# Decoder on one core: keys and values of two cross attentions computed behind the expert tiles, and rows loaded back block by block

## The chip, the cores and the metric

The kernel runs on one core of a Trainium2 chip. A core has five engines that each take their own queue of instructions: TensorE (PE in the profile, with its weight loads as PEld), VectorE (DVE), ScalarE (ACT), GpSimd (POOL) and SyncE (SP), which here issues most of the DMA transfers. The metric is the device time of one execution in microseconds (us). The kernel before has a median of 1467.24 us over 3 runs (1461.73 to 1477.14).

## The reference

The model is a decoder of four layers with layer norms behind each residual sum. The input is 32 sequences of 64 tokens with 128 features, all float32. Each layer has a self attention, a cross attention to a context of the same shape, and a third part that differs: a local transformer (layer 0), routed experts (layers 1 and 2), a linear layer with float8 rounding (layer 3). Every layer runs the same three lines with other functions:

```python
x = _layernorm(x + attn(x))
x = _layernorm(x + xattn(x, ctx_1024))
x = _layernorm(x + ffn(x))
```

The change concerns the cross attentions of layers 2 and 3 and what stands ahead of each layer's self attention. The cross attention of layer 2, cut down (the one of layer 3 has two masks and no output projection):

```python
qh = (q @ Wq.T + bq).reshape(B, S, H, Hd).transpose(0, 2, 1, 3)   # q is x, H = 16, Hd = 8
kh = (k @ Wk.T + bk).reshape(B, S, H, Hd).transpose(0, 2, 1, 3)   # k is ctx_1024
vh = (v @ Wv.T + bv).reshape(B, S, H, Hd).transpose(0, 2, 1, 3)   # v is ctx_1024
attn = softmax(einsum('bhqd,bhkd->bhqk', qh, kh) / sqrt(Hd))
out = einsum('bhqk,bhkd->bhqd', attn, vh).transpose(0, 2, 1, 3).reshape(B, S, D) @ Wo.T + bo
```

Keys and values depend on the context and the weights alone, not on x. The experts of layer 1 send each token to one of eight feed-forward networks; those of layer 2 do the same with room for 80 tokens per expert and weigh the result with the gate's probability.

## The kernel before

**Tiling.** The 2048 tokens lie in 4 blocks of 512 (8 sequences). A block's x has 4 tiles of 128 tokens; xT is the same block turned, with the features on the partitions. The parts of the layers carry names: `l1f` are the experts of layer 1, `l2a` and `l2x` the self and cross attention of layer 2, `l2f` its experts, `l3a` and `l3x` the attentions of layer 3, `l3f` the last linear layer.

**Order.** A list of steps sets TensorE's order by hand: `sp.at(step, place, f)` puts a piece of work at a step and a place in it, and all pieces run sorted by the two. The order of the other engines comes from a scheduler that follows dependencies. SyncE and GpSimd issue the DMAs in their own queues.

**Attention (`attn8`, L618).** A block has 4 score tiles n of 4 sequences and 8 heads each. In a step TensorE makes s(n) from `kx` and q (and, in l2a, the alibi table; in l3a and l3x, a mask); VectorE takes the maximum (L598) and subtracts it; ScalarE makes the exponential (L601). Two steps later TensorE turns p (L612), ScalarE copies it as pT (L614), and TensorE multiplies it with v to o, whose ninth column holds the sum. Between s, the turn of p and o stand, at place 4, the projections of the next block: `prepare` (L640) runs K, Q, V in three successive steps. K is copied by ScalarE (L542, L544) and multiplied with a head mask into two `kx` tiles by GpSimd (L549; this instruction is `self.wide`); for block 0 of a self attention VectorE makes one of the two. V is copied by ScalarE (L564) into one of two constant tiles `v8` with ones in the ninth columns, set up at the start (L392 to L394). Each block ends with the output projection `y`, the residual sum, and a layer norm: statistics on VectorE (L468, L469), rstd on GpSimd (L423, L338), x on GpSimd (L483) or on ScalarE (L490, with `nb`, L488, from VectorE).

**Experts (`sorted_experts` L1301, `capacity_experts` L1441).** 23 tiles of l1f and 8 of l2f run one behind the other. Each scatters its result rows to DRAM by a GpSimd DMA. The last sum of a tile is `y` on VectorE. `wbig`, [128, 8 x 1156] floats, holds the weights of the experts; those of l2f, three transfers for each of the 8 experts (w1 and w2 of 256 KB each, and b2), are asked for while l1f's last tiles run.

**Between the experts and the next attention.** The result rows come back by block as z(b) (`load_after`, L1252). z(0) waits for all scatters. The loads of z(1), z(2) and z(3) are issued behind each other at one step, and wait for `kx` of block 0 as well. `added` sums z and x and normalises: block 0's x half by VectorE, half by ScalarE, all later ones by ScalarE with `nb` from VectorE. `turn_x` (L494) turns x on TensorE and copies xT on ScalarE (L501). In steps counted from the first score of the next self attention, blocks 1, 2 and 3 are added and turned at steps 0, 2 and 4:

```python
back, later = [(n - 4, 3.5), (n, 2), (n + 2, 6), (n + 4, 6)], (n - 1, 2)
```

Of the kernel before, what the change touches and what calls it, by code (L numbers as in the profile page):

```python
# [273 lines left out]
class Decoder:  # L274
# [66 lines left out]
    def setup(self):  # L341
# [48 lines left out]
        for n in range(2):  # L390
            v = self.const([P, BPB, 8, 2, 9], f"v8_{n}")
            nc.gpsimd.memset(v, 0.0)  # L392
            nc.gpsimd.memset(v[0:64, :, :, 0, 8:9], 1.0)
            nc.gpsimd.memset(v[64:128, :, :, 1, 8:9], 1.0)  # L394
            self.v8.append(v)

    def clear(self, sp, first):
# [96 lines left out]
    def turn_x(self, blk, part=(0, TPB)):  # L494
        t0, n = part
        ps = self.ps8("G", "xTps")
        for t in range(n):
            self.nc.tensor.transpose(ps[:, t * P : (t + 1) * P], self.xt[blk][:, t0 + t, :], self.ident)
        if t0 == 0:
            self.xT[blk] = self.const([P, TB], "xT", bufs=5)  # L500
        self.nc.scalar.copy(self.xT[blk][:, t0 * P : (t0 + n) * P], ps[:, 0 : n * P])  # L501


    def attn8_prep(self, blk, w, src, rope, scale, bqs, quick):

# [22 lines left out]
        def q_part():  # L528
            qT = got["q"] = self.q2([P, TB], "q8")
            if rope is not None:  # L530
                turned("wq", "bq", self.xT[blk], rope[:, 0:128], qT)
            elif "bq" in w:
                nc.scalar.activation(qT, proj("wq", self.xT[blk]), AF.Identity, bias=bqs, scale=scale)
            else:
                nc.scalar.mul(qT, proj("wq", self.xT[blk]), scale)

        def k_part():
            kT = self.q2([P, TB], "k8")
            if rope is not None:
                turned("wk", "bk", src(blk), rope[:, 128:256], kT)  # L540
            elif "bk" in w:
                nc.scalar.activation(kT, proj("wk", src(blk)), AF.Identity, bias=w["bk"], scale=1.0)  # L542
            else:
                nc.scalar.copy(kT, proj("wk", src(blk)))  # L544
            got["k"] = []
            for i in range(2):
                kx = self.q4([P, 2, TB], "kx")
                eng = nc.vector if quick and i else nc.gpsimd
                self.wide = eng.tensor_tensor(  # L549
                    out=kx, in0=bc(kT, 1, 2), in1=bc(head[:, 2 * i : 2 * i + 2], 2, TB), op=ALU.mult  # L550
                ).ins
                got["k"].append(kx)

        def v_part():
            x = src(blk)
            p3 = self.ps8("G", "vps").rearrange("p (b h d) -> p b h d", h=8, d=8)
            wv = w["wv"].rearrange("p (h u d) -> p h u d", u=2, d=8)
            for b in range(BPB):
                for u in range(2):
                    self.mm(p3[64 * u : 64 * u + 64, b], x[:, b * S : (b + 1) * S], wv[:, :, u, :])  # L560
            v = got["v"] = self.v8[blk % 2]
            for u in range(2):
                r = slice(64 * u, 64 * u + 64)
                nc.scalar.copy(v[r, :, :, u, 0:8], p3[r])  # L564

        return got, (k_part, q_part, v_part)

# [49 lines left out]

    def attn8(self, sp, base, name, src=None, rope=None, scale=1.0, row=None, mask=(None, None), has_out=True, split=False, number=False):  # L618

# [19 lines left out]

        def prepare(blk, i):  # L640
            if i == 0:
                prep[blk] = self.attn8_prep(blk, setup["w"], src, rope, scale, setup.get("bqs"), quick and blk == 0)
            prep[blk][1][i]()

# [72 lines left out]

        sp.at(base - 4, 3, start)
        for blk in range(NBLK):
            for i in range(3):  # L720
                sp.at(base + 4 * blk - 4 + i, 4, lambda blk=blk, i=i: prepare(blk, i))
            sp.at(base + 4 * blk + 2, 5.5, lambda blk=blk: resid(blk))
# [577 lines left out]

    def sorted_experts(self, sp, name, ready, fetched, tiles, back, later):  # L1301

# [90 lines left out]
        def second(j):  # L1393
# [6 lines left out]
            y = ys[j // 4][:, j % 4, :]  # L1400
            self.tt(y, ps[:, 0:D], w2[:, 4 * P + 4 :], ALU.add)
            at = xg[j // 3].bitcast(U32)[:, j % 3, D : D + 1]
# [15 lines left out]
        def rows_back(b):  # L1418
            z[b] = self.q2([P, TPB, D], "z")
            self.load_after(z[b], self.token_rows(0, b), k["y"] + ([self.wide] if b else []))  # L1420

# [11 lines left out]
        sp.at(tiles[-1][0], tiles[-1][1] + 0.05, lambda: rows_back(0))  # L1433
        for b in range(1, NBLK):
            sp.at(*later, lambda b=b: rows_back(b))
        for b in range(NBLK):
            sp.at(*back[b], lambda b=b: added(b))
            sp.at(back[b][0], back[b][1] + 0.1, lambda b=b: self.turn_x(b))


    def capacity_experts(self, sp, name, ready, fetched, tiles, back, later):  # L1441
        nc = self.nc
# [41 lines left out]
        def second(e):  # L1484
# [23 lines left out]
        def rows_back(b):  # L1508
            z[b] = self.q2([P, TPB, D], "z")
            self.load_after(z[b], self.token_rows(1, b), k["y"] + ([self.wide] if b else []))  # L1510

# [10 lines left out]
        )  # L1522
        sp.at(*fetched, fetch)
# [4 lines left out]
        for b in range(1, NBLK):  # L1528
            sp.at(*later, lambda b=b: rows_back(b))
        for b in range(NBLK):  # L1530
            sp.at(*back[b], lambda b=b: added(b))
            sp.at(back[b][0], back[b][1] + 0.1, lambda b=b: self.turn_x(b))

# [150 lines left out]
def decoder_kernel(ctx: ExitStack, tc: tile.TileContext, ins, at, out):  # L1684
# [63 lines left out]
```

## Time and profile before

| | us |
|---|---|
| median of 3 runs (lowest, highest) | 1467.24 (1461.73, 1477.14) |
| the profiled execution | 1467.96 |
| its span in the profile | 1466.2 |
| TensorE busy | 1228.0 (84%) |
| VectorE, ScalarE, GpSimd busy | 929.0, 694.1, 737.6 |
| mean granted clock of TensorE | 0.889 |

The profile comes from one execution. Its span is the time from the first to the last instruction; 1.8 us lie around it. A row names the source line, the engine, the operation, the tiles out<-in, the shape and how often it ran. "Granted clock" is the share of full speed that TensorE's throttle allowed. In square brackets stand the idle time before a row and the instruction that ended it. The last expert tile of l1f ends at 953, that of l2f at 1212; l2a and l2x lie between the two, l3a, l3x and the last linear layer behind the second.

### The profile page before, as it was taken

To read this page: it belongs to the slowest core of one execution; us is meant where nothing else is said; L and a number is where in the kernel's file an instruction comes from. 1 tells how busy PE (TensorE), PEld (TensorE's weight loads), DVE (VectorE), ACT (ScalarE), POOL (GpSimd) and SP (SyncE) were. 2 spreads that over 40 slices of the span, in tenths; PEclk is the share of its full clock that TensorE was granted. 3 is DMA by queue.
4 is the path that set the end of the run, shared out by engine and by line. 5 is a ranking of instruction groups with operands and counts; after the bars stand their busy time and mean duration, and the time that the engine had idled before them with its cause. 6 is when DMAs were issued, how large, how long until landed. Compare 5 with 4: busy or idle time off the path is not lost. (4 is left out here: it accounts for less than half of the span.)

```text
span 1466.2 us, 36930 instructions
## 1 busy us (share of the span) xinstructions
PE 1228.0 (84%) x16009; PEld 889.8 (61%) x16009; DVE 929.0 (63%) x1831; ACT 694.1 (47%) x1179; POOL 737.6 (50%) x609
## 2 busy tenths in 40 slices
PE   7997888889887898989889995939999853999880
PEld 4775555555555555656667775916677752677670
DVE  5754577777886776666564655635577435676765
ACT  2453444555554554554555542735565312556551
POOL 3534688677785755445542443523355232454531
PEclk9998899999999999999999975969999566999955
DMA  6001010360010000100010002230000001000000
GB/s 231 2 2 24 1 45 1 104 185 2 1 53 1 1 1 2 37 31 2 1 35 32 4 17 60 68 124 2 2 8 5 4 15 32 2 2 3 2 16 14
DMA packets 33714, 43.16 MB, mean 29 GB/s; under 512 B 5946, under 2 KB 27121, under 8 KB 33168
## 3 DMA queue, kind: packets, MB, share of 16 engines
q1 hardware_dynamic: 31536, 38.20, 8.1%
q8 instruction: 126, 2.06, 0.6%
q0 software_dynamic: 2016, 2.60, 0.6%
q14 instruction: 36, 0.29, 0.1%
HBM read 26.63 MB, written 15.56 MB: 29 GB/s over the span
## 5 line engine op out<-in xcount | busy, mean ns | idle before, releaser
L598 DVE TENSOR_REDUCE mx<-s 128x16 f32<-128x1024 f32 x96 | 117.4, 1223 | 127.0 <-PE s L335 125.6
L338 POOL TENSOR_TENSOR turn<-turn,turn 128x1024 f32<-128x1024 f32 x64 | 150.6, 2361 | 92.4 <-DVE turn L338 91.9
L338 DVE TENSOR_TENSOR p<-s,mx 128x1024 f32<-128x1024 f32 (+1 forms) x144 | 158.8, 1103 | 5.0
L614 ACT COPY pT<-ptps 128x512 f32<-128x512 f32 x192 | 104.7, 589 | 92.6 <-PE ptps L612 90.3
L601 ACT ACTIVATE p<-p 128x1024 f32<-128x1024 f32 x96 | 101.6, 1058 | 78.9 <-DVE p L338 77.6
L335 PEld LDWEIGHTS o<-v,pT 128*64 128x64 f32 x3072 | 109.3, 148 | 44.3 <-ACT pT L614 34.6
L549 POOL TENSOR_TENSOR kx<-k,w_const 128x1024 f32<-128x1024 f32 x45 | 85.4, 1917 | 97.8 <-ACT k L542 61.4
L335 PE MATMUL o<-v,pT 128*64 128x18 f32 x3072 | 120.8, 220 | 8.4 <-ACT pT L614 6.2
L335 PE MATMUL s<-kx,q 32*64 32x128 f32 x3072 | 114.6, 286 | 8.0 <-DVE sparts L1558 3.5
L423 POOL TENSOR_SCALAR rstd<-bnmv 128x4 f32<-128x4 f32 (+1 forms) x60 | 16.0, 267 | 198.9 <-DVE bnmv L469 152.5
L612 PE MATMUL ptps<-w_const,p 128*128 128x128 f32 x768 | 115.8, 299 | 0.2 <-ACT c L808 0.2
L335 PEld LDWEIGHTS s<-kx,q 32*64 32x64 f32 x3072 | 89.1, 138 | 44.0 <-issue 40.5
L338 DVE TENSOR_TENSOR turn<-qkps,w_const 128x512 f32<-128x512 f32 (+1 forms) x96 | 75.9, 862 | 53.6 <-PE qkps L335 53.6
L612 PEld LDWEIGHTS ptps<-w_const,p 128*128 128x128 f32 x768 | 96.3, 155 | 9.1 <-issue 8.2
L338 POOL TENSOR_TENSOR rn<-rn,nhalf 128x16 f32<-128x16 f32 x32 | 93.6, 2926 | 2.7
L857 PE MATMUL ropeT<-w_const,turn 128*128 128x128 f32 x512 | 71.1, 285 | 26.2 <-ACT oT L915 12.5
L857 PEld LDWEIGHTS ropeT<-w_const,turn 128*128 128x128 f32 x512 | 58.8, 145 | 39.0 <-ACT oT L915 12.0
L338 DVE TENSOR_TENSOR turn<-qkps,xtab 128x512 f32<-128x512 f32 (+1 forms) x96 | 82.1, 859 | 0.0
L1017 DVE TENSOR_REDUCE rn<-sq 128x16 f32<-128x1024 f32 x32 | 39.0, 1218 | 67.5 <-ACT sq L1013 67.3
L483 POOL TENSOR_SCALAR x<-z,bnmv,rstd 128x128 f32<-128x128 f32 x100 | 79.6, 806 | 2.5
L335 PE MATMUL qkps<-wbig,hT 128*128 128x512 f32 x128 | 72.0, 691 | 10.1 <-POOL hT L993 9.2
L335 PE MATMUL o<-pT,v 64*64 64x64 f32 x2048 | 70.6, 221 | 8.1 <-ACT pT L899 8.1
(331 smaller groups left out, 2731.0 us busy)
## 6 DMA issues: line engine op xcount, KB each, us to landing
sorted_x<-zero SPq DMA_DIRECT2D x9, 990.0 KB, 10.9
wbig<-in_l1f_w_dram SPq DMA_DIRECT2D x4, 1156.0 KB
wbig<-in_l2f_w_dram SPq DMA_DIRECT2D x16, 256.0 KB, 5.3
wbig<-in_l0f_dram SPq DMA_DIRECT2D x2, 1561.0 KB
z<-token_y SPq DMA_DIRECT2D x8, 256.0 KB, 2.9
wbig<-in_l1a_dram SPq DMA_DIRECT2D x1, 1856.0 KB
xsorted<-sorted_x SPq DMA_DIRECT2D x23, 66.0 KB, 1.8
xT<-in_xT_dram SPq DMA_DIRECT2D x4, 256.0 KB, 4.7
```

Of the source, the lines that this page charges most:

```text
L335: self.nc.tensor.matmul(out, lhsT=lhsT, rhs=rhs, start=start, stop=stop)
L338: (eng or self.nc.vector).tensor_tensor(out=out, in0=a, in1=b, op=op)
L423: nc.gpsimd.tensor_scalar(r[:, :n], var, EPS, None, ALU.add)
L483: eng.tensor_scalar(x[:, t0 + t, :], z[:, t0 + t, :], mv[:, t, 0:1], r[:, t : t + 1], ALU.subtract, ALU.mult)
L549: self.wide = eng.tensor_tensor(out=kx, in0=bc(kT, 1, 2), in1=bc(head[:, 2 * i : 2 * i + 2], 2, TB), op=ALU.mult).ins
L598: nc.vector.tensor_reduce(mx, s3, AX.X, ALU.max)
L601: nc.scalar.activation(pr, pr, AF.Exp)
L612: self.nc.tensor.transpose(ps[:, j, :], flat[:, c : c + P], self.ident)
L614: self.nc.scalar.copy(o, ps)
L857: self.nc.tensor.transpose(pt[:, j * P : (j + 1) * P], f[:, j * P : (j + 1) * P], self.ident)
L1017: nc.vector.tensor_reduce(rn, sq, AX.X, ALU.add)
```

## The change

Four things are changed together.

1. K and V of l2x's blocks 0 to 2 and of l3x's blocks 0 to 3 are made directly behind the last expert tile, in the same step (`ahead`). They are written into `wbig`, over expert weights that are no longer needed: 1152 floats of V and 512 of K for each block. The zeros and ones of V are set there by GpSimd (even blocks) or VectorE (odd blocks) behind the last expert's sum. In the attention itself `k_part` only makes `kx` from the K that is there, and `v_part` does nothing.
2. The self attentions l2a and l3a are `held`: K and Q of blocks 1 to 3 stand one step later, so that Q (place 4.5) shares a step with V (place 4).
3. The rows of blocks 1 to 3 are loaded, added and turned at steps of their own. z(1) waits for ScalarE's copy of xT(0) (`self.turned`) instead of `kx`; z(2) waits for `kx` of block 1, z(3) for `kx` of block 2. Blocks 1, 2 and 3 are added at steps -1, 3 and 7 and turned at 1, 5 and 9.
4. The weights of l2f are asked for in three groups: experts 5 to 7, then 0 and 1, then, two steps later, 2 to 4. The groups lie so that the places which K and V of l2x occupy are filled later. In the built order of the SyncE queue 7 transfers of 256 KB and 4 of b2 stand ahead of z(0), and the other 9 and 4 behind z(3).

The diff, cut to its core (`capacity_experts` has the same changes to `rows_back` and to the steps of its blocks as `sorted_experts`):

```diff
         self.v8 = []
         for n in range(2):
             v = self.const([P, BPB, 8, 2, 9], f"v8_{n}")
-            nc.gpsimd.memset(v, 0.0)
-            nc.gpsimd.memset(v[0:64, :, :, 0, 8:9], 1.0)
-            nc.gpsimd.memset(v[64:128, :, :, 1, 8:9], 1.0)
+            self.set_ones(v, nc.gpsimd)
             self.v8.append(v)
+    def set_ones(self, v, eng):
+        first = eng.memset(v, 0.0)
+        eng.memset(v[0:64, :, :, 0, 8:9], 1.0)
+        eng.memset(v[64:128, :, :, 1, 8:9], 1.0)
+        return first.ins
     def clear(self, sp, first):
...
             self.nc.tensor.transpose(ps[:, t * P : (t + 1) * P], self.xt[blk][:, t0 + t, :], self.ident)
         if t0 == 0:
             self.xT[blk] = self.const([P, TB], "xT", bufs=5)
-        self.nc.scalar.copy(self.xT[blk][:, t0 * P : (t0 + n) * P], ps[:, 0 : n * P])
-    def attn8_prep(self, blk, w, src, rope, scale, bqs, quick):
+        self.turned = self.nc.scalar.copy(self.xT[blk][:, t0 * P : (t0 + n) * P], ps[:, 0 : n * P]).ins
+    def attn8_prep(self, blk, w, src, rope, scale, setup, quick):
...
             if rope is not None:
                 turned("wq", "bq", self.xT[blk], rope[:, 0:128], qT)
             elif "bq" in w:
-                nc.scalar.activation(qT, proj("wq", self.xT[blk]), AF.Identity, bias=bqs, scale=scale)
+                nc.scalar.activation(qT, proj("wq", self.xT[blk]), AF.Identity, bias=setup["bqs"], scale=scale)
             else:
                 nc.scalar.mul(qT, proj("wq", self.xT[blk]), scale)
         def k_part():
-            kT = self.q2([P, TB], "k8")
-            if rope is not None:
-                turned("wk", "bk", src(blk), rope[:, 128:256], kT)
-            elif "bk" in w:
-                nc.scalar.activation(kT, proj("wk", src(blk)), AF.Identity, bias=w["bk"], scale=1.0)
-            else:
-                nc.scalar.copy(kT, proj("wk", src(blk)))
+            kT = got.get("kT")
+            if kT is None:
+                kT = self.q2([P, TB], "k8")
+                keys(kT)
             got["k"] = []
             for i in range(2):
                 kx = self.q4([P, 2, TB], "kx")
...
                 ).ins
                 got["k"].append(kx)
+        def keys(kT):
+            if rope is not None:
+                turned("wk", "bk", src(blk), rope[:, 128:256], kT)
+            elif "bk" in w:
+                nc.scalar.activation(kT, proj("wk", src(blk)), AF.Identity, bias=w["bk"], scale=1.0)
+            else:
+                nc.scalar.copy(kT, proj("wk", src(blk)))
         def v_part():
+            if "v" not in got:
+                got["v"] = self.v8[blk % 2]
+                values(got["v"])
+        def values(v):
             x = src(blk)
             p3 = self.ps8("G", "vps").rearrange("p (b h d) -> p b h d", h=8, d=8)
             wv = w["wv"].rearrange("p (h u d) -> p h u d", u=2, d=8)
             for b in range(BPB):
                 for u in range(2):
                     self.mm(p3[64 * u : 64 * u + 64, b], x[:, b * S : (b + 1) * S], wv[:, :, u, :])
-            v = got["v"] = self.v8[blk % 2]
             for u in range(2):
                 r = slice(64 * u, 64 * u + 64)
                 nc.scalar.copy(v[r, :, :, u, 0:8], p3[r])
-        return got, (k_part, q_part, v_part)
+        return got, (k_part, q_part, v_part), keys, values
     def attn8_scores(self, blk, pp, gg, prep, mask):
...
                 nc.vector.tensor_scalar(setup["bqs"], w["bq"], scale, None, ALU.mult)
         def prepare(blk, i):
+            if i == 0 and blk not in prep:
+                prep[blk] = self.attn8_prep(blk, setup["w"], src, rope, scale, setup, quick and blk == 0)
+            prep[blk][1][i]()
+        def early(blk, i):
+            n = BPB * 8 * 2 * 9
+            at = blk * (n + TB)
             if i == 0:
-                prep[blk] = self.attn8_prep(blk, setup["w"], src, rope, scale, setup.get("bqs"), quick and blk == 0)
-            prep[blk][1][i]()
+                prep[blk] = self.attn8_prep(blk, self.w[name], src, None, scale, setup, False)
+                v = prep[blk][0]["v"] = self.big[:, at : at + n].rearrange("p (b h u d) -> p b h u d", h=8, u=2, d=9)
+                self.after(self.set_ones(v, nc.vector if blk % 2 else nc.gpsimd), [self.summed])
+                return
+            got, _, keys, values = prep[blk]
+            if i == 1:
+                got["kT"] = self.big[:, at + n : at + n + TB]
+                keys(got["kT"])
+            else:
+                values(got["v"])
         def score(n):
             m, gg = divmod(n, 2)
...
             elif i == 1:
                 self.norm(blk, zs.pop(blk), True, number)
-        sp.at(base - 4, 3, start)
+        sp.at(base - 4, 2.4 if held else 3, start)
+        if ahead:
+            step, place, m = ahead
+            for i in range(3):
+                for blk in range(m):
+                    sp.at(step, place + 0.1 * i, lambda blk=blk, i=i: early(blk, i))
         for blk in range(NBLK):
             for i in range(3):
-                sp.at(base + 4 * blk - 4 + i, 4, lambda blk=blk, i=i: prepare(blk, i))
+                n = base + 4 * blk - 4
+                at = (n + 1 + (i + 1) // 2, 4 + i % 2 / 2) if held and blk else (n + i, 4)
+                sp.at(*at, lambda blk=blk, i=i: prepare(blk, i))
             sp.at(base + 4 * blk + 2, 5.5, lambda blk=blk: resid(blk))
             if halved(blk):
                 sp.at(base + 17, 5.5, lambda blk=blk: self.turn_x(blk, (0, 2)))
...
         return self.token_y[i][b * TB : (b + 1) * TB, :].rearrange("(t p) d -> p t d", p=P)
-    def sorted_experts(self, sp, name, ready, fetched, tiles, back, later):
+    def sorted_experts(self, sp, name, ready, fetched, tiles, back):
...
             if j % 4 == 0:
                 ys[j // 4] = self.q2([P, 4, D], "ysorted")
             y = ys[j // 4][:, j % 4, :]
-            self.tt(y, ps[:, 0:D], w2[:, 4 * P + 4 :], ALU.add)
+            self.summed = nc.vector.tensor_tensor(out=y, in0=ps[:, 0:D], in1=w2[:, 4 * P + 4 :], op=ALU.add).ins
             at = xg[j // 3].bitcast(U32)[:, j % 3, D : D + 1]
             self.scatter(self.token_y[0], y, at, k["y"], [], NT - 1)
             weights(j + AHEAD)
...
         def rows_back(b):
             z[b] = self.q2([P, TPB, D], "z")
-            self.load_after(z[b], self.token_rows(0, b), k["y"] + ([self.wide] if b else []))
+            self.load_after(z[b], self.token_rows(0, b), k["y"] + [[], [self.turned], [self.wide], [self.wide]][b])
         def added(b):
             self.tt(z[b], z[b], self.xt[b], ALU.add)
...
         for j, at in enumerate(tiles):
             sp.at(*at, lambda j=j: tile_(j))
         sp.at(tiles[-1][0], tiles[-1][1] + 0.05, lambda: rows_back(0))
-        for b in range(1, NBLK):
-            sp.at(*later, lambda b=b: rows_back(b))
         for b in range(NBLK):
-            sp.at(*back[b], lambda b=b: added(b))
-            sp.at(back[b][0], back[b][1] + 0.1, lambda b=b: self.turn_x(b))
-    def capacity_experts(self, sp, name, ready, fetched, tiles, back, later):
+            if b:
+                sp.at(*back[b][0], lambda b=b: rows_back(b))
+            sp.at(*back[b][1], lambda b=b: added(b))
+            sp.at(*back[b][2], lambda b=b: self.turn_x(b))
+    def capacity_experts(self, sp, name, ready, fetched, tiles, back):
         nc = self.nc
         k = dict(done=[], y=[])
         xg, st, ys, z = {}, {}, {}, {}
         NS = NEXP * CAP
         wts = [self.big[:, e * EROW : (e + 1) * EROW] for e in range(NEXP)]
-        def fetch():
-            for e, w in enumerate(wts):
+        def fetch(experts):
+            for e in experts:
+                w = wts[e]
                 self.load(w[:, 0 : 4 * P], self.ins[name + "_w1"][e])
                 self.load(w[:, 4 * P : 8 * P].rearrange("p (c d) -> p c d", d=P), self.ins[name + "_w2"][e])
                 self.load(w[0:CAP, 8 * P : 8 * P + D], self.ins[name + "_b2"][0, e * D : (e + 1) * D].partition_broadcast(CAP))
...
             if e % 4 == 0:
                 ys[e // 4] = self.q2([P, 4, D], "eo")
             y = ys[e // 4][0:CAP, e % 4, :]
-            self.tt(y, ep, w[0:CAP, 8 * P : 8 * P + D], ALU.add)
+            self.summed = nc.vector.tensor_tensor(out=y, in0=ep, in1=w[0:CAP, 8 * P : 8 * P + D], op=ALU.add).ins
             at = xg[e // 3].bitcast(U32)[0:CAP, e % 3, D : D + 1]
             self.scatter(self.token_y[1], y, at, k["y"], self.cleared, NT - 1)
...
     ready, n = n + 8, n + 21
     tiles = [(n, 0.1 + 0.1 * j) for j in range(NTL)]
     n = n + 4
-    back, later = [(n - 4, 3.5), (n, 2), (n + 2, 6), (n + 4, 6)], (n - 1, 2)
-    k.sorted_experts(sp, "l1f", ready, (n - 16, 7), tiles, back, later)
-    k.attn8(sp, n, "l2a", scale=s8, row=rows["l2a_bo"], mask=("heads", "alibi"))
-    k.attn8(sp, n + 16, "l2x", c, scale=s8, row=rows["l2x_bo"], split=True, number=True)
+    back = [
+        (None, (n - 4, 3.5), (n - 4, 3.6)), ((n - 4, 3.7), (n - 1, 5), (n + 1, 2.5)),
+        ((n + 1, 4.5), (n + 3, 6), (n + 5, 3.5)), ((n + 5, 4.5), (n + 7, 6), (n + 9, 3.5)),
+    ]
+    k.sorted_experts(sp, "l1f", ready, (n - 16, 7), tiles, back)
+    k.attn8(sp, n, "l2a", scale=s8, row=rows["l2a_bo"], mask=("heads", "alibi"), held=True)
+    ahead = (n - 4, 2.6, 3)
+    k.attn8(sp, n + 16, "l2x", c, scale=s8, row=rows["l2x_bo"], split=True, number=True, ahead=ahead)
     late(sp, n + 12, "l3a")
     late(sp, n + 28, "l3x")
     n = n + 16
     ready, n = n + 8, n + 21
     tiles = [(n, 0.1 + 0.1 * j) for j in range(NEXP)]
     n = n + 4
-    back, later = [(n - 4, 3.5), (n, 2), (n + 2, 6), (n + 4, 6)], (n - 1, 2)
-    k.capacity_experts(sp, "l2f", ready, (n - 14, 7), tiles, back, later)
-    k.attn8(sp, n, "l3a", rope=k.c["r3"], row=rows["l3a_bo"], mask=("all", "causal"))
-    k.attn8(sp, n + 16, "l3x", c, scale=s8, row=rows["l3x_bv"], mask=("batch", "mask3"), has_out=False, split=True)
+    back = [
+        (None, (n - 4, 3.5), (n - 4, 3.6)), ((n - 4, 3.7), (n - 1, 5), (n + 1, 2.5)),
+        ((n + 1, 4.5), (n + 3, 6), (n + 5, 3.5)), ((n + 5, 4.5), (n + 7, 6), (n + 9, 3.5)),
+    ]
+    fetched = [(n - 14, 7, (5, 6, 7)), (n - 14, 7.1, (0, 1)), (n - 12, 7, (2, 3, 4))]
+    k.capacity_experts(sp, "l2f", ready, fetched, tiles, back)
+    k.attn8(sp, n, "l3a", rope=k.c["r3"], row=rows["l3a_bo"], mask=("all", "causal"), held=True)
+    ahead = (n - 4, 2.6, 4)
+    k.attn8(sp, n + 16, "l3x", c, scale=s8, row=rows["l3x_bv"], mask=("batch", "mask3"), has_out=False, split=True, ahead=ahead)
     k.fp8_linear(sp, n + 16 + 9, (n - 4, 1.5))
     with (
```

More of the change, by code (lines that the diff above doesn't have):

```diff
@@ L616, in attn8_turn, with attn8 @@
         return out
-    def attn8(self, sp, base, name, src=None, rope=None, scale=1.0, row=None, mask=(None, None), has_out=True, split=False, number=False):
+    def attn8(self, sp, base, name, src=None, rope=None, scale=1.0, row=None, mask=(None, None), has_out=True, split=False, number=False, ahead=None, held=False):
         nc = self.nc
@@ L1509, in rows_back @@
             z[b] = self.q2([P, TPB, D], "z")
-            self.load_after(z[b], self.token_rows(1, b), k["y"] + ([self.wide] if b else []))
+            self.load_after(z[b], self.token_rows(1, b), k["y"] + [[], [self.turned], [self.wide], [self.wide]][b])
         def added(b):
@@ L1522, in capacity_experts @@
         )
-        sp.at(*fetched, fetch)
+        for step, place, experts in fetched:
+            sp.at(step, place, lambda experts=experts: fetch(experts))
         sp.at(ready + 12, 8.1, loads)
@@ L1527, in capacity_experts @@
         sp.at(tiles[-1][0], tiles[-1][1] + 0.05, lambda: rows_back(0))
-        for b in range(1, NBLK):
-            sp.at(*later, lambda b=b: rows_back(b))
         for b in range(NBLK):
-            sp.at(*back[b], lambda b=b: added(b))
-            sp.at(back[b][0], back[b][1] + 0.1, lambda b=b: self.turn_x(b))
+            if b:
+                sp.at(*back[b][0], lambda b=b: rows_back(b))
+            sp.at(*back[b][1], lambda b=b: added(b))
+            sp.at(*back[b][2], lambda b=b: self.turn_x(b))
     def masks(self):
```

## The prediction

> **What bounds the kernel now.** I read the table of windows first (per stretch: start:end, length, busy us of TensorE, its weight loads, VectorE, ScalarE, GpSimd, then granted clock, DMA share, GB/s):
>
> ```profile
> 953.50:997.00 43.50, 21.23 (x208) 10.82 (x208) 16.64 (x51) 14.19 (x27) 14.41 (x14) 0.69 0.32 102
> 1050.00:1110.00 60.00, 59.06 (x1082) 46.57 (x1074) 43.10 (x71) 38.32 (x61) 28.64 (x30) 1.00 0.02 6
> ...
> 1212.50:1260.00 47.50, 22.58 (x207) 12.09 (x206) 27.99 (x83) 13.04 (x24) 14.18 (x15) 0.68 0.09 24
> 1320.00:1380.00 60.00, 59.00 (x1104) 45.19 (x1100) 43.16 (x69) 39.10 (x60) 31.53 (x31) 1.00 0.01 3
> ```
>
> In l2x (1050) and l3x (1320) TensorE is 98% busy at full clock: each microsecond of matmul taken out of there shortens the run. In the two stretches behind the experts TensorE is half idle and a chain of small steps sets the time. The timeline of TensorE (start, length, idle before and its releaser) shows the holes:
>
> ```profile
> 953.08 0.39 PE L335 MATMUL bvps<-w_l2a 128*128 128x128 f32 x2
> 966.58 1.29 PE L498 MATMUL xTps<-w_const,x 128*128 128x128 f32 x4 [13.12 <-ACT x L490]
> ...
> 982.87 1.64 PE L498 MATMUL xTps<-w_const,x 128*128 128x128 f32 x4 [6.65 <-ACT x L490]
> ...
> 1224.36 1.29 PE L498 MATMUL xTps<-w_const,x 128*128 128x128 f32 x4 [11.86 <-ACT x L490]
> ...
> 1244.70 1.64 PE L498 MATMUL xTps<-w_const,x 128*128 128x128 f32 x4 [7.04 <-ACT x L490]
> ```
>
> The first hole is scatter, z(0), norm; the second is z(1), which waits for kx(0), its add and norm. The SyncE queue shows the issues:
>
> ```profile
> 959.05 0.38 SPq L1252 DMA_DIRECT2D z<-token_y  x1
> ...
> 972.69 1.48 SPq L1252 DMA_DIRECT2D z<-token_y  x3
> ```
>
> **1. Relief in l2x and l3x.** K and V of l2x blocks 0-2 and of l3x blocks 0-3 leave these rows:
>
> ```profile
> 1091.25 1.02 PE L335 MATMUL proj<-ctxT,w_l2x 128*128 128x512 f32 x2
> 1092.20 1.11 PE L335 MATMUL o<-v,pT 128*64 128x18 f32 x32
> ...
> 1359.49 1.15 PE L335 MATMUL vps<-w_l3x,ctxT 128*64 128x64 f32 x32
> ...
> 1363.04 1.09 PE L612 MATMUL ptps<-w_const,p 128*128 128x128 f32 x8
> 1364.42 1.37 PE L335 MATMUL o<-v,pT 128*64 128x18 f32 x32 [0.29 <-ACT pT L614]
> ```
>
> Start to start, K costs 0.95 and V 0.98: 1.93 a block. But work between the turn of p and o hides the wait for ScalarE's pT: in l3x a step with V takes 4.57 (1358.47 to 1363.04), a step with nothing there 4.25. So a block without filler yields 0.32 for V and 0.24 for K (4.98 to 4.74). l2x keeps other fillers: 3 x 1.93 = 5.8. In l3x, blocks 0 and 1 still have l3a's output products as cover, 3.9; blocks 2 and 3 give 1.1. Sum 10.8. VectorE then fills 88% of an l2x block's period instead of 79% (13.8 of 15.6, was 17.6), so I take 9.8, bounds 6 and 10.8.
>
> **2. The same work in the holes.** Warm, it is 3 x 1.93 = 5.8 in a hole of 13.1, and 7.7 in one of 11.9; ScalarE's copies end near 962 and 1223, before x(0) at 966 and 1224. GpSimd's memsets (1.06 + 2 x 0.21 per block, by the rows of the set-up) are 3.0 in a gap before rstd. I count 0. The bounds: TensorE all cold would be 15.4 in the second hole, +3.5; VectorE's memsets (blocks 1, 3) are in no row; at GpSimd's price, the nearest, they fill the same gap. They wait for the last expert sum; queued behind them are rstd on GpSimd, idle 8.98 before 963.87, and the add of z(0) on VectorE, which comes later still.
>
> **3. The weights' queue.** The issue of z(0) came 4.16 after the last scatter beside the l2f weights, 1.33 at the second boundary without them. Seven large loads instead of nine stand ahead of it: -2, bounds 0 and -2.8. The other nine wait for the last readers of K and V and start near 1094-1136, needed at 1191: covered, with weight loads elsewhere beside a 92-100% busy TensorE. Behind the waits of z(2) and z(3) on the SyncE queue stand only these and w_l3x, none due before 1191. If they hold up instruction fetch near 1130, +5 at most.
>
> **4. Block 1's rows come sooner.** I replayed by hand the built order of each engine with the rows' durations. z(1) now waits for ScalarE's copy of xT(0), which ends at 968.5, not for kx(0) and the issue at 972.69; its load lands near 971.4, VectorE's add and statistics and GpSimd's rstd (behind its half of kx(0), to 974.4) end near 977, ScalarE's x(1) near 979. Meanwhile s(1), which needs block 0 alone, follows s(0) directly in TensorE's order; before, it stood behind the turn of x(1) and its wait of 6.65. So s(2) ends near 985 instead of 994.7. At o(1) 3.8 are given back: ScalarE's four x(2), whose load waits for kx(1), stand ahead of pT(1). The score s(5) ends at 1003.55 instead of 1011.9, -8.35, with 1.95 of TensorE work still owed (turns of x(2) and x(3), K of block 2). At the second boundary the same way -7.7 (1266.0, was 1273.7), 2.9 owed.
>
> **5. Block 3's rows come later, and this is the new wait.** Before, all z came early. Now z(3) waits for kx of block 2, and the norm of block 3 is queued behind l2a's (l3a's) own first norm on GpSimd:
>
> ```profile
> 1031.44 3.75 POOL L549 TENSOR_TENSOR kx<-k,w_const 128x1024 f32<-128x1024 f32 x2 [5.97 <-ACT k L542]
> ...
> 1043.43 0.23 POOL L423 TENSOR_SCALAR rstd<-bnmv 128x4 f32<-128x4 f32 x1 [7.01 <-DVE bnmv L469]
> 1043.75 1.04 POOL L338 TENSOR_TENSOR rstd<-rstd,nhalf 128x4 f32<-128x4 f32 x1
> 1044.89 3.14 POOL L483 TENSOR_SCALAR x<-z,bnmv,rstd 128x128 f32<-128x128 f32 x4
> ```
>
> From the end of s(5), t0: turn of p, turn of x(2), its copy, K and its copy take 4.35, kx(2) 3.75, so z(3) is issued at t0+8.1 and lands at t0+11.0 (2.9 from issue to add, as above). GpSimd does resid meanwhile, then the norm of l2a's block 0, whose statistics come near t0+13.8: rstd 1.3, x 3.14; then rstd of block 3, done at t0+19.7. In the built order VectorE's nb(3) stands ahead of the maximum of s(7), and ScalarE's four x(3) (0.2 and 1.7) ahead of pT(5) (0.65): o(5) starts at t0+22.25. Without them it would be t0+14.95: 7.3 of stall. At the second boundary GpSimd has l3a's rotary adds too, t0+24.35 against 15.1: 9.2. From s(5) to s(8) it makes 25.9 instead of 16.2, and 27.2 instead of 14.85: +9.7 and +12.35; 1.1 is still owed each time. Net of 4 and 5: -8.35 + 9.7 + 1.1 = +2.45, and -7.7 + 12.35 + 1.1 = +5.75; together +8.2. Bounds: without the stalls -8.3, see the rivals; nothing makes them longer but a later z(3).
>
> **6. The clock behind a stall.** Stalls of 7 and 9 us put TensorE on half clock. What this case shows:
>
> ```profile
> 852.33 0.92 PE L335 MATMUL s<-kx,q 32*64 32x128 f32 x23 [0.62 <-issue]
> 853.74 1.80 PE L612 MATMUL ptps<-w_const,p 128*128 128x128 f32 x8
> ...
> 1386.45 0.61 PE L335 MATMUL y<-kq,xq 128*128 128x128 bf16 x4 [4.02 <-DVE xq L338]
> ```
>
> The turn of p takes 1.80 instead of 1.09: after a stall of 0.62 for some 10 us, after one of 4.02 until 1426. The Trainium skill ("TensorE: Matmul & The Clock Gate", "What's actually happening") says that a cold array is back at full clock after about 3.4 us of sustained work. By that, a stall costs half of 3.4, 1.7 each, 3.4 in sum; by the rows, 8-10 us at half clock cost 4-5 each. The measurement decides: I take 4 each, +8.
>
> **Sum.** -9.8 - 2 + 8.2 + 8 = +4.4, against the profiled execution's 1467.96 (span 1466.2 and 1.8 around it): 1472.4. It stands 0.7 above the median of 1467.24, so 1471.7 to be compared with the median; I say **1471**, within the 1% (about 14.7 us) that a measurement of this kernel can tell from no change.
>
> **Rivals.**
> *The stall of step 5 doesn't arise* (0.26). For it: VectorE and ScalarE are 57% and 56% busy from 997 to 1050, so x(3) can be done with little delay if z(3) lands before the order reaches it, and the first 8 us of my chain rest on GpSimd's kx, whose spans are rough. Against it: seven dependent steps, each from a row. Without 7.3, 9.2 and 8: -20, so 1447.
>
> *Slower: the half clock stays* (0.25). After the wait of 4.02 the clock stayed at half for 40 us, with steps of 7 to 7.8 instead of 4.25, since a step without dense projections is broken by pT waits. The last steps of l2a have no projections, and l2x's have lost theirs. Each further cold step costs 2.7; from four on (+11 on top of +4.4) it decides. Six, three behind each stall, give +16: 1488. For it: the two stalls are longer than 4.02. Against it: after holes of 13.1 and 6.65 in l2a the clock was back within about 8 us.
>
> *It doesn't do what it says*: K and V made ahead could lengthen the holes by 3.5 and the pT wait could eat all of l3x's relief (5.0): +8.5, 1480; within the likeliest case's range.
>
> **How the numbers follow.** Likeliest (0.49): 1471, 1465 to 1482: below by 1.0, 0.8 and 4.6 (the good ends of 1, 3 and 6), above by 3.8, 3.5, 2 and 2 (the bad ends of 1, 2, 3 and 6). The first rival spreads as much about 1447, the second about 1488; 1444 to 1490 leaves out some third of each, under 2 in 10. Faster by over 1% is under 1452.6, nearly all of the first rival: 0.25. Slower is over 1481.9: 0.26, with the tail of the likeliest. Within: 0.49.
>
> **What would show it.** Step 1: blocks of l2x near 15.6 instead of 17.6 apart, no proj from ctxT before block 3. Step 2: proj and vps rows inside both holes, x(0) transposes at the same distance from the last expert. Step 3: z(0) some 2 sooner. Step 4: s(5) about 8 sooner. Step 5: o(5) with idle of 7 and 9 before it, released by pT behind four x(3). Step 6: granted clock about 0.85 in the 20 us after. I am wrong if z(3) lands before l2a's own norm reaches GpSimd, if the compiled queues run in another order than built, or if half clock outlasts 10 us.

## The result

The changed kernel takes 1489.03 us (median of 4 runs, 1485.41 to 1494.13), the kernel before beside it 1467.85: ratio 1.0125, 95% interval 1.0088 to 1.0162. It is 21 us slower. The likeliest case, 1465 to 1482, did not hold; the number lies at the end of the second rival. The profiled execution took 1492.29 (span 1490.5).

Split at the same instructions, the two profiles compare like this (us; the last column from the steps of the prediction; half of step 6's 8 stands in each of the two rows marked *, and the rows take the 10.8 that step 1 added up, not the 9.8 that it took):

| stretch | before | after | difference | predicted |
|---|---|---|---|---|
| last l1f product to turn of x(0) | 13.5 | 12.9 | -0.6 | -2 |
| turn of x(0) to end of s(5), l2a | 45.3 | 39.5 | -5.8 | -8.35 |
| s(5) to s(8) | 16.2 | 28.0 | +11.8 | +9.7 |
| s(8) to the start of l2x's set-up | 24.1 | 36.8 | +12.7 | +1.1 and +4* |
| l2x and l2f | 160.0 | 156.5 | -3.5 | -5.8 |
| last l2f product to turn of x(0) | 12.2 | 12.2 | 0 | 0 |
| turn of x(0) to end of s(5), l3a | 49.3 | 47.9 | -1.4 | -7.7 |
| s(5) to s(8) | 14.8 | 32.2 | +17.4 | +12.35 and +4* |
| s(8) to the first s of l3x | 39.3 | 41.1 | +1.8 | -0.8 |
| l3x to the first product of l3f | 58.6 | 56.4 | -2.2 | -3.1 |
| rest | 79.8 | 80.2 | +0.4 | 0 |

They sum to about +30.6; the part up to l1f's end was 6.4 shorter in this execution. It varies by chance: in five more profiles of kernels with the same code up to there it ended between 947.3 and 952.8, here at 946.7.

The timeline of TensorE of the changed kernel, as shown of before (start, length, idle before and its releaser):

```profile
959.66 1.29 PE L503 MATMUL xTps<-w_const,x 128*128 128x128 f32 x4 [7.02 <-ACT x L495]
...
971.67 1.26 PE L503 MATMUL xTps<-w_const,x 128*128 128x128 f32 x4
...
1021.20 1.96 PE L335 MATMUL o<-v,pT 128*64 128x18 f32 x32 [7.07 <-ACT pT L628]
...
1272.72 0.66 PE L717 MATMUL aT<-w_const,a 128*128 128x128 f32 x2 [3.71 <-DVE a L338]
...
1308.07 1.96 PE L335 MATMUL o<-v,pT 128*64 128x18 f32 x32 [9.03 <-ACT pT L628]
```

The work made ahead fills some 6 of the 13 us of the first hole, and the wait of 6.65 for x(1) is gone. In its place stand idle times of 7.07 and 9.03 before o(5), where the prediction had 7.3 and 9.2, and one of 3.71 for VectorE's a. The timeline of all engines shows the chain of the first:

```profile
1007.32 0.36 SPq L1290 DMA_DIRECT2D z<-token_y  x1
...
1010.23 0.69 DVE L338 TENSOR_TENSOR z<-z,x 128x512 f32<-128x512 f32 x1 [1.44 <-DMA z<-token_y]
...
1014.33 3.14 POOL L488 TENSOR_SCALAR x<-z,bnmv,rstd 128x128 f32<-128x128 f32 x4
...
1018.83 0.16 DVE L493 SCALAR_TENSOR_TENSOR nb<-bnmv,rstd 128x4 f32<-128x4 f32 x1 [6.26 <-POOL rstd L338]
...
1019.03 1.65 ACT L495 ACTIVATE x<-z,nb,rstd 128x128 f32<-128x128 f32 x4 [7.60 <-DVE nb L493]
...
1020.58 1.04 ACT L628 COPY pT<-ptps 128x512 f32<-128x512 f32 x2
```

From s(5)'s end at 999.12 these are +8.2 (issue of z(3)), +11.1 (its add), +19.7 (nb), +22.1 (o(5)). GpSimd normalises l2a's own block 0 (3.14) first; VectorE waits 6.26 for rstd(3) with the maximum of s(7) behind it; ScalarE waits 7.60 with pT(5) behind it.

What the likeliest case did not have is the length of the half clock. The table of windows of the changed kernel around the wait (columns as before; the third number from the right is the granted clock):

```profile
1013.00:1021.00 8.00, 1.12 (x12) 0.86 (x8) 2.07 (x3) 1.97 (x5) 5.71 (x8) 0.81 0.00 0
1021.00:1031.00 10.00, 9.80 (x95) 7.46 (x96) 4.21 (x7) 3.96 (x7) 0.00 (x0) 0.50 0.01 2
1031.00:1053.00 22.00, 21.32 (x193) 14.71 (x191) 7.39 (x15) 6.62 (x11) 3.75 (x2) 0.52 0.00 1
1053.00:1060.00 7.00, 6.69 (x112) 4.46 (x110) 2.40 (x3) 3.00 (x5) 6.70 (x8) 1.00 0.01 2
```

TensorE is 97% busy from 1021 to 1053, and stays at half clock until 1052 all the same. The clock had fallen at 1018, 3 us before o(5). Lengths of half clock below are counted from where the clock falls: here 34 us, 31 of them behind o(5).

### The profile page after: what moved, and what is told of

It is laid out like the page before. It is cut to its first block, busy times and chain, and to the rows that moved or that the text cites. A ratio compares the mean times of both kernels' runs of the same rounds, so it can differ in the third digit from the quotient of the medians.

```text
span 1490.5 us, 36980 instructions
## 1 busy us (share of the span) xinstructions
PE 1259.3 (84%) x16009; PEld 909.4 (61%) x16009; DVE 935.8 (63%) x1840; ACT 693.5 (47%) x1179; POOL 741.8 (50%) x621
## 4 chain that ended last, share of the span: by engine, by line
PE 52%; DVE 18%; POOL 13%; ACT 9%; issue 5%; DMA 3%; SPq 0%; POOLq 0%; ACTq 0%; DVEq 0%
PE s L335 10%; PE o L335 9%; PE qkps L335 5%; PE ptps L626 5%; DVE turn L338 5%; PE proj L335 4%; POOL turn L338 4%; PE y L335 4%; PE ropeT L895 3%; POOL rstd L338 2%; DVE p L338 2%; DVE rn L1055 2%; ACT pT L628 2%; PE xTps L503 2%; POOL rn L338 2%
## 5 line engine op out<-in xcount | busy, mean ns | idle before, releaser
L335 PE MATMUL s<-kx,q 32*64 32x128 f32 x3072 | 118.8, 294 | 7.5 <-DVE sparts L1598 2.7
L626 PE MATMUL ptps<-w_const,p 128*128 128x128 f32 x768 | 120.2, 307 | 0.3 <-ACT c L846 0.2
L335 PEld LDWEIGHTS s<-kx,q 32*64 32x64 f32 x3072 | 92.6, 143 | 43.7 <-issue 39.8
L335 PEld LDWEIGHTS o<-v,pT 128*64 128x64 f32 x2176 | 79.7, 151 | 48.5 <-ACT pT L628 32.2
L626 PEld LDWEIGHTS ptps<-w_const,p 128*128 128x128 f32 x768 | 100.0, 160 | 9.9 <-issue 8.6
L335 PE MATMUL o<-v,pT 128*64 128x18 f32 x2176 | 88.0, 222 | 21.0 <-ACT pT L628 19.9
L551 POOL TENSOR_TENSOR kx<-k,w_const 128x1024 f32<-128x1024 f32 x31 | 59.2, 1928 | 91.8 <-ACT k L560 56.4
L895 PE MATMUL ropeT<-w_const,turn 128*128 128x128 f32 x512 | 70.1, 283 | 22.3 <-ACT oT L953 8.7
```

The lines of the kernel that those rows point to most:

```text
L335: self.nc.tensor.matmul(out, lhsT=lhsT, rhs=rhs, start=start, stop=stop)
L551: self.wide = eng.tensor_tensor(out=kx, in0=bc(kT, 1, 2), in1=bc(head[:, 2 * i : 2 * i + 2], 2, TB), op=ALU.mult).ins
L626: self.nc.tensor.transpose(ps[:, j, :], flat[:, c : c + P], self.ident)
L895: self.nc.tensor.transpose(pt[:, j * P : (j + 1) * P], f[:, j * P : (j + 1) * P], self.ident)
```

## The experiments

Three theories were set against each other: A, the waits behind block 3's rows and the half clock that they set off carry the loss; B, the half clock comes anyway, from steps without dense projections; C, the loss lies in the work made ahead and the late weights. Ratios are to the kernel before, run alongside on the same chip. The edits are cut to the lines that differ.

**Block 3's rows early.** In both `back` lists:

```diff
-((n + 5, 4.5), (n + 7, 6), (n + 9, 3.5)),
+((n + 1, 4.6), (n + 3, 6.1), (n + 9, 3.5)),
```

> The changed kernel with block 3's rows loaded and added directly behind block 2's (steps 1 and 3, waiting for kx of block 1); TensorE's and SyncE's orders stay as they are. Theory A (the wait of o(5) for the norm of block 3, and the half clock it sets off, carry the loss): both idle times of 7.1 and 9.0 us before o(5) go, and with them 31 us and 7 us at half clock, about 14 and 3: 1489 - 16 - 17 = about 1456, below the kernel before. Theory B (the stall alone, the half clock comes anyway from the steps without dense projections): 1489 - 16 = 1473, with half clock still standing between s(8) and s(13). Theory C (the loss lies in the work made ahead or the late weights): 1485 or more.

1468.28 us, ratio 1.0012 (0.9991 to 1.0033): the whole loss against the kernel before is gone, and no more. The stalls before o(5) and the half clock behind them are away: from the turn of x(0) to l2x's set-up 85.1 instead of 104.3. At the second boundary the wait for a stays, since block 2's norm still stands ahead of it on VectorE, and half clock follows from 1255 to 1272:

```profile
1255.99 0.66 PE L717 MATMUL aT<-w_const,a 128*128 128x128 f32 x2 [3.46 <-DVE a L338]
1256.45 1.91 PE L626 MATMUL ptps<-w_const,p 128*128 128x128 f32 x8
```

From the turn of x(0) to l3x this kernel takes 112.0; before 103.5, after 121.2. These 8.5 us are most of why it lands at 1468, not at A's 1456.

**Keys and values ahead alone.** Rows, adds, turns and projections at the steps of before:

```diff
-((n - 4, 3.7), (n - 1, 5), (n + 1, 2.5)),
-((n + 1, 4.5), (n + 3, 6), (n + 5, 3.5)), ((n + 5, 4.5), (n + 7, 6), (n + 9, 3.5)),
+((n - 1, 2), (n, 2), (n, 2.1)),
+((n - 1, 2), (n + 2, 6), (n + 2, 6.1)), ((n - 1, 2), (n + 4, 6), (n + 4, 6.1)),
-[[], [self.turned], [self.wide], [self.wide]][b]
+[[], [self.wide], [self.wide], [self.wide]][b]
-held=True
```

> The changed kernel with rows, adds, turns and projections of the self attentions at the steps of the kernel before; only keys and values made ahead, and the weights asked for in three groups, stay. Theory A: the relief alone, 9.8 by my sum and about 10 by the trace of the changed kernel (3.5 and 2.6 outside the self attentions, 1.9 inside each): 1468 - 10 = 1458. Theory C: no faster than the kernel before, 1468 or more, with a longer hole behind the experts or a longer stretch of l2f.

1462.78, ratio 0.9961 (0.9943 to 0.9979): faster, so theory C falls, but by 4 between the medians (3 to 8 by the ratio), not by 10. The kernel with block 3's rows early is still 5.5 slower than this one, so the rest of the change to the rows costs time too.

**Rows alone.** `ahead` left out, the weights asked for in one group:

```diff
-fetched = [(n - 14, 7, (5, 6, 7)), (n - 14, 7.1, (0, 1)), (n - 12, 7, (2, 3, 4))]
+fetched = [(n - 14, 7, range(NEXP))]
-split=True, number=True, ahead=ahead)
+split=True, number=True)
-has_out=False, split=True, ahead=ahead)
+has_out=False, split=True)
```

> The changed kernel without the keys and values made ahead and with the weights asked for at once, as before; rows block by block and the held projections stay. Theory A: the loss is all here, 1489 + 10 = 1499, with idle times of 7 and 9 us before o(5). Theory C: 1468 or less, since block 1's rows come 4 us sooner.

1494.72, ratio 1.0172 (1.0130 to 1.0213). The rows carry the loss. Against the changed kernel the relief is worth 5.7, but the two intervals overlap, so this number alone shows little. One thing I had not expected: in this profile the half clock of l2a's stall (7.69) lasts 14 us instead of 34, with the same instructions in TensorE's order there.

**Unread matmuls in the wait.** In `values`, ahead of o(5) of l2a and l3a:

```diff
+if held and n == 5:
+    junk = self.ps8("G", "fill8")
+    for i in range(22 if rope is None else 28):
+        self.mm(junk.rearrange("p (h k) -> p h k", k=S), self.identb, bc(self.causal, 1, 8))
```

> The changed kernel with matmuls that nobody reads (22 in l2a, 28 in l3a, 128x512 bf16, about 0.27 us each) put into TensorE's order between the turn of p and o(5); nothing else moves. It takes the idle time off TensorE, but o(5) starts no sooner. If the idle time sets off the half clock: no half clock behind o(5), 1489 - 17 = about 1472. If the clock falls for another reason, such as the kind of matmuls in those steps: 1489, as the changed kernel.

1493.82, ratio 1.0154 (1.0100 to 1.0208): no gain. But the matmuls took 0.22 each, not 0.27, so idle times of 2.40 and 2.85 were left, and half clock came with them for 31 and 17 us (timeline of TensorE of this kernel):

```profile
1026.04 1.96 PE L335 MATMUL o<-v,pT 128*64 128x18 f32 x32 [2.40 <-ACT pT L628]
...
1300.98 6.20 PE L335 MATMUL fill<-causal,identb 128*128 128x512 bf16 x28
1310.03 1.96 PE L335 MATMUL o<-v,pT 128*64 128x18 f32 x32 [2.85 <-ACT pT L628]
```

It settled only that waits as short as these did not keep the full clock.

**The changed kernel again.** No edit.

> The changed kernel once more, unchanged, for a second profile. The idle times of 7 and 9 us before o(5) are set by the order of the queues and should stay within some tenths. If the length of the half clock behind them is set by the work alone, it is 34 and 14 us again; if it depends on where the clock's windows fall (the kernel with only the rows changed had 13 us at half behind the same idle time), it differs by whole windows of about 3.4 us.

1481.23 in its one run. The stall in l2a is 7.07 again (timeline of TensorE of that execution):

```profile
1021.43 1.95 PE L335 MATMUL o<-v,pT 128*64 128x18 f32 x32 [7.07 <-ACT pT L628]
```

But the half clock ends at 1031, after 14 us instead of 34 (windows of that execution):

```profile
1021.00:1031.00 10.00, 9.57 (x90) 7.23 (x92) 4.25 (x6) 3.96 (x7) 0.00 (x0) 0.50 0.01 2
1031.00:1060.00 29.00, 27.91 (x435) 19.80 (x434) 14.79 (x29) 13.57 (x22) 14.33 (x12) 0.99 0.01 2
```

From o(5) to l2x's set-up it takes 33.8, the first profile 42.7: the same kernel, 8.9 apart. In l3a the wait for a was 3.12 with 24 us of half clock, and since TensorE came later the one before o(5) only 5.63. So the order alone does not set the length of the half clock. The second stall shows the same: with 9.03 or 9.04 of waiting before o(5) in l3a, the half clock lasted 14 us in the first profile of the changed kernel, and 24 in those of the rows alone and of the dense matmuls below.

**The wait filled completely.** As above, with more of them:

```diff
-for i in range(22 if rope is None else 28):
+for i in range(34 if rope is None else 42):
```

> As the kernel with unread matmuls before o(5), with enough of them to leave TensorE no idle time there (34 and 42, about 0.22 us each, where 22 and 28 left 2.4 and 2.9). If idle time sets off the half clock and an unbroken stretch holds the full clock: o(5) starts as late as in the changed kernel, the half clock behind it is gone, and the time is 1489 - 20 = about 1469. If the steps behind it are too thin to hold the clock in any case: half clock within 10 us behind o(5), 1489.

1477.04, ratio 1.0052 (1.0028 to 1.0077), 12 less than the changed kernel (11 by the ratios, whose intervals lie apart), where 20 less were expected. o(5) starts no sooner, 22.3 behind the end of s(5) (22.1 in the changed kernel), but at full clock (timeline of TensorE of this kernel):

```profile
1018.81 1.09 PE L626 MATMUL ptps<-w_const,p 128*128 128x128 f32 x8
1019.74 7.50 PE L335 MATMUL fill<-causal,identb 128*128 128x512 bf16 x34
1027.17 1.20 PE L335 MATMUL o<-v,pT 128*64 128x18 f32 x32
```

No half clock follows in l2a: from o(5) to l2x's set-up 29.5. Against 42.7 and 33.8 the half clock behind this one stall cost 13.2 and 4.3 in the two profiles. Theory B falls for these stretches: the same thin steps run at full clock when no idle time precedes them.

**Dense matmuls behind the wait.** 16 unread 128x512 matmuls directly behind o(5) of l2a:

```diff
+if held and rope is None and n == 5:
+    junk = self.ps8("G", "fill8")
+    for i in range(16):
+        self.mm(junk.rearrange("p (h k) -> p h k", k=S), self.identb, bc(self.causal, 1, 8))
```

> The changed kernel with 16 unread 128x512 matmuls directly behind o(5) in l2a, where the clock is at half. If broad matmuls bring the clock back, and the narrow ones of a step without projections don't: full clock within 7 us of their start instead of 31 us behind o(5); the idle time before o(5) stays at 7. Cost about 5 us of filler, gain up to 11: 1484 or so. If only time counts: half clock until the step with V and Q, as in the changed kernel.

```profile
1025.63 1.95 PE L335 MATMUL o<-v,pT 128*64 128x18 f32 x32 [7.06 <-ACT pT L628]
1027.52 6.34 PE L335 MATMUL fill<-causal,identb 128*128 128x512 bf16 x16
1033.70 1.34 PE L335 MATMUL s<-alibi,ident 128*128 128x512 bf16 x4
```

The clock is back at the end of the 6.34 us. That agrees with the expectation, but doesn't decide it: the changed kernel without them had come back after 14 us too in one of its profiles, 10 us behind o(5), and here it was 7. The one run took 1493.51.

**A fill in the tail.** The kernel with keys and values ahead alone, plus unread matmuls in TensorE's waits for the first two products of l3f:

```diff
+if t0 in (0, 4):
+    junk = self.ps8("G", "fill8")
+    for i in range(20 if t0 == 0 else 12):
+        self.mm(junk.rearrange("p (h k) -> p h k", k=S), self.identb, bc(self.causal, 1, 8))
```

> The kernel with only the keys and values made ahead, with unread matmuls in TensorE's waits for the first two products of the last linear layer (20 and 12). In the kernels before and after alike TensorE runs at half clock from there on, 40 us and more, with steps of 7 to 8 us instead of 4.25. If the fill holds the clock: four steps at 4.3 to 5 instead of 7.2, about 10 us less, 1453. If it doesn't: 1463 as without it, or some us more.

1460.80, ratio 0.9942 (0.9921 to 0.9962), hardly less than without. Two steps run at full clock; then TensorE, now faster, meets a new wait of 3.10 for pT, and the clock falls there:

```profile
1388.58 1.96 PE L335 MATMUL o<-wbig,pT 128*64 128x18 f32 x32 [3.10 <-ACT pT L628]
```

**Block 1 early, blocks 2 and 3 as before.** On the kernel with keys and values ahead alone:

```diff
-((n - 1, 2), (n, 2), (n, 2.1)),
+((n - 4, 3.7), (n - 1, 5), (n + 1, 2.5)),
-[[], [self.wide], [self.wide], [self.wide]][b]
+[[], [self.turned], [self.wide], [self.wide]][b]
-if held and blk else (n + i, 4)
+if held and blk == 1 else (n + i, 4)
+held=True   (l2a and l3a)
```

> Keys and values made ahead, block 1's rows early as in the change (z(1) behind xT(0), its turn behind s(1), its projections one step later), but blocks 2 and 3 loaded together behind kx of block 0 and turned where the kernel before turns them. If the loss of the change lies in block 3's (and, at the second boundary, block 2's) late rows alone: block 1's gain of 4 to 8 at each boundary stays and nothing is given back, 1463 - 8 = about 1455. If the norms of blocks 2 and 3 then stand ahead of pT(0) and pT(1) on ScalarE and cost what block 1 gains: 1463, as with the keys and values alone; with a new idle time of over 3 us and its half clock, 1470.

1450.12 beside 1454.91 for the kernel before, run alongside; in the earlier experiments it gave 1467, so only the ratio compares: 0.9952 (0.9931 to 0.9974), no different from keys and values ahead alone. No idle time of 7 us and no wait for a is left, but the norms of blocks 2 and 3 stand ahead of pT(1) on ScalarE; o(1) waits 1.83 with half clock behind it (timeline of TensorE of this kernel):

```profile
989.22 1.45 PE L335 MATMUL o<-v,pT 128*64 128x18 f32 x32 [1.83 <-ACT pT L628]
990.60 2.23 PE L335 MATMUL s<-alibi,ident 128*128 128x512 bf16 x4
```

So block 1's early rows gain nothing net: the middle case of the expectation.

**The same with fills.** Added to it: 30 and 18 unread matmuls ahead of the turn of x(0), 20 and 12 ahead of the first two products.

```diff
+sp.at(n - 4, 3.55, lambda: k.fill(30))   # behind l1f; 18 behind l2f
+if t0 in (0, 4):
+    self.fill(20 if t0 == 0 else 12)
```

> The same with unread matmuls where TensorE waits: 30 and 18 ahead of the turn of x(0) at the two boundaries, 20 and 12 ahead of the first two products of the last linear layer. If an unbroken stretch holds the clock: the turn of x(0), the first projections and s(0) run at full clock, 3 to 4 us less at each boundary, and 2 to 6 at the end: about 10 less than without. If the clock falls in the later waits all the same: no more than 3 less.

1438.13 beside 1454.91: ratio 0.9869 (0.9839 to 0.9899), the fastest of all, 1.3% below the kernel before. It is 12.0 below the kernel without the fills. Of this the profile gives 3.1 between the turn of x(0) in l3a and l3x (102.0 instead of 105.1), 3.3 in the tail and 1.2 in l2a; 5.5 lie in l2x and l2f, where the edit changes nothing and the half clock was shorter (10 and 31 us instead of 55). Whether that follows from the edit or is chance was not tested, so not all of the 12 is shown to come from the fills.

## Why the prediction was right or wrong

**Step 5, the new wait: right**, in place, cause and size: 7.07 and 9.03 for 7.3 and 9.2, o(5) at t0+22.1 for t0+22.25. Moving block 3's rows away removed both. The first rival (the stall doesn't arise) did not come true.

**Step 6, the clock: this is the step that failed.** That a stall is followed by half clock was right; how much of it was wrong. It charged 4 for each of two stalls, by rows with 8 to 10 us at half clock. Behind the first the half clock lasted 34 us; taking the stall and the owed work (+9.7 and +1.1) from what was measured (+11.8 and +12.7) leaves 13.7, and the filled wait confirms 13.2. Behind the second it lasted 14 us, 7 of them behind o(5), and cost some 3: the five rows from o(5) on take 6.9 there, and 3.8 from 1322.89 on, at full clock. Here the charge of 4 was about right. A third charge was missing: the wait of 3.71 for VectorE's a in l3a, which the prediction does not name, came with 17 us at half clock. It cost its own 3.71 and, by an estimate of the same kind from the rows up to 1287.73, some 3.6 ahead of the end of s(5), where block 1's gain was lost, and 2.9 behind it. Together that is some 23 of half clock instead of 8, and 3.7 of waiting. It is most of the miss.

The second rival had named the row for this, the 40 us behind a wait of 4.02, and ended at 1488. That its number is so near is in part luck. It supposed three half-clock steps behind each stall, at 2.7 each. Found were some three behind the first, which cost 13.7 in one profile and 4.3 in another, less than one behind the second, and some two behind the wait for a. I gave it 0.25 because after the holes of 13 and 6.65 the clock had come back within 8 us. There the broad projections of a new block follow at once, and behind o(5) the steps hold few of them. That this makes the difference is not shown: in the second profile of the changed kernel the clock came back at 1031, and the first projection behind o(5) started at 1037.

The wait for a in l3a is in seven profiles. In four it was 2.90 to 3.05 and the half clock lasted 3.4 us; in three it was 3.12, 3.46 and 3.71, with 24, 17 and 17 us. So a wait longer by a tenth of a microsecond went with much more half clock; seven profiles don't make a threshold of it.

The rule weighed there, from the Trainium skill ("TensorE: Matmul & The Clock Gate", "What's actually happening"), gave an estimate of 3.4 in sum, further off still. Its window is in these traces: the half-clock stretches are near 3.4, 7, 10, 14, 17, 24 and 34 us, multiples of the 3.4 that the page states. It calls the window free-running, so that a shift of the work against it can make a stretch differ. How that makes six windows of difference behind the same stall (14 and 34 us) stays open. But "sustained" is not busy time as the profile counts it: 31 us at 97% busy did not bring the clock back. That the narrow matmuls of s and o count for too little is my reading. It was not isolated: each step of l2a also has four 128x512 matmuls for the alibi table, and the second profile, which came back on the same rows, speaks against it as the only reason.

**Step 1, the relief: right in direction, half in size.** 9.8 was taken; the runs give 4.0 (keys and values alone); the 5.7 of the changed kernel against rows alone is within the noise of the two. l3x behind its first score gave 2.2 in every kernel with the relief, of 3.1. l2x and l2f gave 3.5 of 5.8 in the first profile (4.0 up to l2x's 14th score product, which lies ahead of any half clock there): each bare step now waits 0.24 for pT, and VectorE, fuller, made TensorE wait once more for a:

```profile
1098.99 0.41 PE L717 MATMUL aT<-w_const,a 128*128 128x128 f32 x2 [0.60 <-DVE a L338]
```

Block 0's share in l3a doesn't show at all. In the profile of the keys and values alone two bare steps there each dropped to half clock for one window, with no more than 0.3 us of idle in them:

```profile
1302.01 1.37 PE L335 MATMUL o<-v,pT 128*64 128x18 f32 x32 [0.28 <-ACT pT L628]
...
1305.27 1.92 PE L626 MATMUL ptps<-w_const,p 128*128 128x128 f32 x8
```

**Step 4: right in direction.** -5.8 for -8.35 in l2a. Block 1's x came as foretold, its turn 12.0 behind that of x(0) for 12.4. But from there to the end of s(2) it took 9.3 instead of 6, at half clock from 974 to 984, and the 3.8 foretold at o(1) was a wait of 0.48: one error hid part of the other. In l3a it was -1.4 for -7.7, lost to the wait for a and its clock. **Step 2: right**, no cost: the holes are as long as before. **Step 3: small**, -0.6 for -2: z(0) was issued 3.68 behind the last scatter instead of 4.16. The late weights delayed nothing that the profile shows.

## What to carry to other kernels

Cost a new wait of TensorE with the clock behind it, not with its own length alone: here 7 us of waiting cost 4 to 13 more, and waits of 2 to 4 us came with half clock too. Moving broad matmuls out of a busy stretch was worth less than their own time: 4.0 where 10.8 was added up, since the bare steps waited for pT, and some of them fell to half clock. When a norm is moved, ask on each in-order engine which ready instruction will stand behind its last wait.

## What the runs showed of the hardware

A stretch that is 97% busy, mostly with narrow matmuls, stayed at half clock for 31 us behind a stall of 7.07, and the same kernel left it 10 us behind the same stall in another execution. Unread 128x512 bf16 matmuls, back to back at 0.22 us each, held the full clock through waits of 7 to 9 us where they left no gap; where they left gaps of 2.40 and 2.85 us the half clock came all the same. They took 12 us off the changed kernel. Put into the holes behind the experts and the waits of the last layer, together with the keys and values made ahead and block 1's early rows, they made the fastest kernel, 1.3% below the kernel before.

The spread between runs of one kernel goes with the clock as well: in 39 runs of the kernel before the mean granted clock lay between 0.879 and 0.893, and the slowest run (1477.03) had the lowest; the fastest (1462.18) had 0.892.
